# Swin attention and a dynamic convolution: the parameter stage and step 2 rearranged

## The chip, the cores and the metric

The kernel runs on one core of a Trainium2 chip. A core has a matrix engine (TensorE, "PE" in the profile, its weight loads "PEld"), three engines for elementwise work (VectorE "DVE", ScalarE "ACT", GpSimd "POOL"), a Sync engine that here only issues transfers ("SPq" is its queue), and 16 DMA engines that carry the transfers. Every engine runs its own instructions in the order in which they were written, and waits where one needs what another engine or a transfer has yet to deliver. The metric is the time of one execution on the device in microseconds (us), as a median of runs. Everything is in float32.

## The reference

The input is a batch of 16 images of 192 channels, 56 x 56. The first layer is a Swin block: layer norm over channels, windows of 7 x 7 on an image rolled by 3, attention with 6 heads of 32, a projection, a residual; then a second layer norm, an MLP 192 -> 768 -> 192 with GELU, and a residual. The second layer makes four 3 x 3 taps per channel and image out of the pooled image and convolves with them.

```python
h = _ln(transpose(x), norm1_g, norm1_b)
win = windows(roll(h, (-3, -3)))                       # 64 windows of 49 tokens
q, k, v = split(win @ qkv_w + qkv_b)
attn = softmax(q * SCALE @ k.T + bias[None] + mask)    # bias: relative positions; mask: rolled edges
x1 = x + roll(unwindows(attn @ v @ proj_w + proj_b), (3, 3))
y = gelu(_ln(x1, norm2_g, norm2_b) @ fc1_w + fc1_b) @ fc2_w + fc2_b
x2 = x1 + y
wt = (relu(batchnorm(mean(x2) @ w1.T)) @ w2.T + b2) * MASK     # per image and channel
out = depthwise_conv(x2, wt) + bias
```

## The kernel before, in words

**Tiling.** Channels lie on the partitions: `x0` holds channels 0 to 127, `x1` channels 128 to 191 twice, for the two halves of an image. A step `i` takes one window row of each half of an image, 784 tokens; an image has 4 steps (`STEPS`), all 64 (`NS`). The loop `for i in range(2, NS + 2)` is a software pipeline: in one turn it does the MLP of step i - 2, the attention of step i, the q, k, v of step i + 1 and the norm statistics of steps i + 2 and i - 1. What stands ahead of the loop, from line 852 on, loads parameters, folds norm gains, means and shifts into the weights, and takes steps 0, 1 and 2 through the first stages by hand. The change lies there.

**Order.** `tc.manual_schedule()` leaves every engine's instructions in the order of the text. Waits are put in between by the framework, by tile. Tiles of one tag share buffers.

**Names.** A norm is taken in two parts. `norm_squares` or `norm_folded` make squares (the latter adds the three pieces of a token on POOL first: `xs` is filled by two transfers, `copies`; `sums`, `squares` and `fold` follow). `norm_stats` gets means by matmuls with `sel` into `st`, `st_a`, `st_b` or `st_c`; `norm_vars`, `norm_root` and a reciprocal make 1/deviation in `dev`. `norm_spread` writes it to DRAM (`rows`) and reads it back on all partitions (`dv`). Step 0's is spread by matmuls into `pd` instead ("dv" in the profile). `norm1_scale` multiplies into the window tiles `win`, `norm2_scale` into `yn`.

`shift` multiplies a norm's shift with raw weights, a row of 576 (qkv) or 768 (fc1) numbers in one partition. `turn_row` turns pieces of it into columns, one matmul for each 64 or 128. These are added to `qkb`, `bv` (for qkv) and `f1b` (for fc1).

`biases(r, e)` makes one of four attention bias tables, six VectorE additions of `rel_r` and `mask_t`; `r` is 1 for the last step of an image, which is step 3 at the earliest. `attention_scores` adds a table to the scores and makes softmax in `top` (maximum, exponential) and `share` (sum, division); `attention_turn` transposes it into `pt`, copied to `prt`. `attention_v` makes v in two blocks of PSUM, `attention_v_out` copies these into `vbd`, one half on VectorE and one on ScalarE. `attention_qk` returns four copies, q, k and two for the rest, to be called later. `mlp_first` writes `ph`, and has the statistics `st` in its middle; `mlp_wide` and `mlp_narrow` write `pf`. PSUM is four pairs of banks, which all these tiles share in turn.

Of the kernel before, what the change touches and what calls it, by code (L numbers as in the profile page):

```python
# [19 lines left out]
N = WS * WS  # L20
# [16 lines left out]
def tile_swin_then_dynamic_conv(  # L37
# [45 lines left out]
    def banks(name, k):  # L83
        return psum.tile([128, 2, 512], F32, tag=f"pair{k}", name=name)

    def mm(dst, lhs, rhs, start, stop):
        nc.tensor.matmul(dst, lhs, rhs, start=start, stop=stop, skip_group_check=True)  # L87
# [105 lines left out]
    def turn_row(dst, row, lo, n):  # L193
        mm(dst, row[:, lo : lo + n], ident[0:1, 0:1], True, True)

# [9 lines left out]
    qkb = const.tile([128, 3], F32, tag="qkb", name="qkb")  # L205
    wp0 = const.tile([128, DIM], F32, tag="wp0", name="wp0")
# [3 lines left out]
    f1b = const.tile([128, NFC], F32, tag="f1b", name="f1b")  # L210
    wf2 = const.tile([128, NFC, DIM], F32, tag="wf2", name="wf2")
# [27 lines left out]
    mask_t = one.tile([PW, 2, 2, N], F32, tag="prt", name="mask_t", bufs=4)  # L239
# [104 lines left out]
    def norm_vars(keys, st, tag="dev"):  # L344

        lo, hi = min(keys) * 32, max(keys) * 32 + 32
        d = one.tile([128, T], F32, tag=tag, name=f"dev_{keys[min(keys)]}")
        part = d[64 + lo : 64 + hi]
        nc.scalar.activation(part, st[lo:hi, 0, :T], AF.Square)
        nc.vector.tensor_tensor(part, st[64 + lo : 64 + hi, 0, :T], part, ALU.subtract)  # L350
        return part, d
# [4 lines left out]
    def norm_spread(keys, part, tags=("dv1", "sq01"), order=(1, 0)):  # L356

        rows = dram.tile([2 * len(keys), T], F32, tag="rows", name=f"rows_{keys[min(keys)]}")
        nc.sync.dma_start(rows, part[::16])
        out = {}  # L360
        for side in order:
            if side not in keys:
                continue
            v = one.tile([128, 2, T], F32, tag=tags[side], name=f"dv_{keys[side]}")
            at = 2 * (side - min(keys))
            nc.sync.dma_start(
                v,
                rows[at : at + 2].rearrange("(o h) t -> o h t", o=1).broadcast_to([128, 2, T]),
            )
            out[side] = v  # L370
        return out
# [141 lines left out]
    def attention_v_out(pvs):  # L513

        for blk, pv in enumerate(pvs):
            src = pv.rearrange("p h (w n) -> p h w n", w=2)[:, :, :, 0:DIM]
            src = src.rearrange("p h w (g j d) -> p h w g j d", j=2, d=HD)
            for h, copy in enumerate((nc.vector.tensor_copy, nc.scalar.copy)):
                for s in range(2):
                    for j in range(2):  # L520
                        dst = vbd[h][j * 64 : j * 64 + N].rearrange(
                            "p (b w s) g (j d) -> p b w s g j d", b=2, s=2, j=2
                        )[:, blk, :, s, :, j, :]
                        copy(dst, src[s * 64 : s * 64 + N, h, :, :, j, :])  # L524
# [352 lines left out]
    load_rows(*images[0], 0, 3 * WS, HALF, nc.sync)  # L877
    nc.sync.dma_start(rawf[:, 0], fc1_w[0:C0])
    rows2(rawf[:, 1], fc1_w, nc.sync)
# [9 lines left out]
    nc.sync.dma_start(mask_t, win_mask)  # L889
# [31 lines left out]
    g1, be1, bq, bk, bv = columns(*rows1, 2, nc.vector.tensor_copy)  # L921
    nc.vector.memset(kbd, 0.0)
# [16 lines left out]
    part, _ = norm_vars(keys, st, "o")  # L939
# [4 lines left out]
    pq = banks("qkb_p", 2)  # L944
    row = shift(pq, raw, 3 * DIM, be1, "qkb_row")
    pq = pq[:, 0, 384:390]
    norm_squares("1_2", 2, 1, nc.scalar)

    pd = banks("dv_0", 3)
    for h in range(2):  # L950
        pick_row = ident[64:96, 64 + h * 16 : 65 + h * 16].broadcast_to([32, 128])
        mm(pd[:, h, :T], pick_row, part, True, True)
    fold_center(wqkv, 3 * DIM, pm)
# [8 lines left out]
    for _, c, at, lo, n, _ in parts:  # L962
        turn_row(pq[at : at + n, c : c + 1], row, lo, n)
    g2, be2, f2b, pb, cb = columns(*rows3, 1, nc.scalar.copy)
    norm1_scale(0, pd[:, :, :T], nc.vector)
    for dst, c, at, _, n, b in parts:
        nc.vector.tensor_tensor(dst, b, pq[at : at + n, c : c + 1], ALU.add)
# [3 lines left out]


    st = banks("st_b", 0)
    keys = {0: "1_1", 1: "1_2"}
    norm_stats(keys, {0: 1, 1: 2}, st)
    part, _ = norm_vars(keys, st)
# [5 lines left out]
    for r in range(2):  # L982
        for e in range(2):
            biases(r, e)
# [35 lines left out]
    pbp, f1p, pt = pv[:, 0, 384:386], pv[:, 0, 392 : 392 + NFC], pv[:, 1, 384:512]  # L1020
    top(0)
    row = shift(pv, rawf, HID, be2, "f1b_row")

    def rows_to_columns():
        for f in range(NFC):
            turn_row(f1p[:, f : f + 1], row, f * 128, 128)

    qs[1], outs = attention_qk(1, 2, 0, 1, rows_to_columns, nc.vector)
# [29 lines left out]
    outs[3]()  # L1058
    o = attention_rows(0, attention_values(0, prts, 3, 2))
# [36 lines left out]
    dvs.update(norm_spread(keys, part))  # L1096
# [9 lines left out]
    v_whole()  # L1106
    copies, sums_, squares, fold = norm_folded("1_4", 4, 0)
    copies()
    squares(nc.scalar)()
    table(AF.Gelu)  # L1110
    sums_((0,))
    yns[0] = norm2_scale(0, dvs.pop(1), True)
    sums_((1,))
    fold()
    attention_v_out(pvs)
# [245 lines left out]
```

## Time and profile before

The three runs took 3045.3, 3045.47 and 3048.54 us. The profiled execution has a span of 3044.4 us.

| Engine | busy, us | share |
| --- | --- | --- |
| TensorE (PE) | 3022.7 | 99% |
| VectorE (DVE) | 2156.3 | 71% |
| ScalarE (ACT) | 1948.7 | 64% |
| GpSimd (POOL) | 1343.5 | 44% |

In the page, a group's line gives code line, engine, operation, tiles written and read, count, busy time and mean of one, and idle time of its engine before it with what ended most of that. In a timeline, each line starts with the time from the start of the span and the duration, and ends with the idle time before it in brackets. Lines of a matmul are those of a helper, L87, so that tiles tell them apart; a float32 matmul shows as two records. In a table of stretches, each engine has its busy time and, in brackets, the number of its instructions; then come the TensorE clock that was granted (1 is full), the mean busy share of the DMA engines, and what they moved.

### The profile page before, as it was taken

How to read it: one execution, taken by the hardware profiler on the slowest of the kernel's cores; microseconds unless marked ns; L12 is line 12 of the kernel's file. 1: busy time of each engine (PE TensorE's matmuls, PEld its weight loads, DVE VectorE, ACT ScalarE, POOL GpSimd, SP SyncE). 2: the span in 40 equal slices, each digit the busy share in tenths (PEclk: the TensorE clock that was granted, in tenths of full speed). 3: DMA queues.
4: the chain of work that ended last, by engine and by line, in shares of the span. 5: the costliest groups of instructions: out<-in, count | busy, mean ns of one | idle time of the engine just before them, and what ended most of it. 6: DMA issues, size and time to landing. Idle time of an engine off the chain costs nothing.

```text
span 3044.4 us, 62149 instructions
## 1 busy us (share of the span) xinstructions
PE 3022.7 (99%) x25174; PEld 1891.4 (62%) x25174; DVE 2156.3 (71%) x3841; ACT 1948.7 (64%) x3159; POOL 1343.5 (44%) x1269
## 2 busy tenths in 40 slices
PE   9999999999999999999999999999999999999998
PEld 5666666666666666666666666666666666666654
DVE  8656677676686676776866867767767668668664
ACT  4666676666666666766766667667666667666563
POOL 6444534444435445344444444453454444444422
PEclk9999999999999999999999999999999999999999
DMA  4112121111211112121121211212111121211101
GB/s 111 33 31 59 41 75 41 43 60 46 73 38 62 52 44 68 44 72 36 41 67 47 70 36 52 65 41 78 39 47 56 46 73 38 62 52 43 33 30 56
DMA packets 68711, 159.89 MB, mean 53 GB/s; under 512 B 11250, under 2 KB 35288, under 8 KB 66504
## 3 DMA queue, kind: packets, MB, share of 16 engines
q1 hardware_dynamic: 66766, 153.84, 16.7%
q8 instruction: 199, 3.26, 0.4%
q0 software_dynamic: 1360, 1.26, 0.3%
q14 instruction: 88, 0.72, 0.1%
q10 hardware_dynamic: 298, 0.81, 0.1%
HBM read 92.24 MB, written 38.93 MB: 43 GB/s over the span
## 4 chain that ended last, share of the span: by engine, by line
PE 97%; DVE 1%; DMA 1%; POOL 1%; issue 0%; ACT 0%; SPq 0%; POOLq 0%; DVEq 0%; ACTq 0%
PE ph L87 26%; PE pf L87 25%; PE pv L87 8%; PE pp L87 8%; PE po L87 6%; PE pq L87 5%; PE pt L581 5%; PE sc L87 4%; PE pk L87 4%; PE pe L87 4%; PE st L87 2%; PE pc L87 0%; DMA wp<-in_L_conv_proj_w_dram 0%; PE pb_p L87 0%; DVE e L559 0%
## 5 line engine op out<-in xcount | busy, mean ns | idle before, releaser
L87 PE MATMUL pf<-hid,wf 128*128 128x392 f32 (+1 forms) x3072 | 802.6, 493 | 1.5 <-DVE e L552 1.5
L87 PE MATMUL ph<-yn,wf 128*128 128x392 f32 (+1 forms) x3072 | 799.3, 497 | 1.8 <-ACT vbd L524 1.5
L568 POOL TENSOR_TENSOR prob<-e,tot 113x588 f32<-113x588 f32 x256 | 298.3, 1176 | 1098.8 <-DVE tot L567 1098.6
L87 PEld LDWEIGHTS ph<-yn,wf 128*128 128x128 f32 (+1 forms) x3072 | 426.4, 188 | 346.6 <-issue 47.5
L87 PEld LDWEIGHTS pf<-hid,wf 128*128 128x128 f32 (+1 forms) x3072 | 386.2, 164 | 301.3 <-issue 120.2
L524 ACT COPY vbd<-pv 49x192 f32<-49x192 f32 x512 | 160.5, 313 | 575.9 <-DVE vbd L524 571.4
L717 DVE SCALAR_TENSOR_TENSOR x<-pf,cols,x 128x784 f32<-128x784 f32 (+1 forms) x128 | 106.2, 830 | 506.3 <-PE pf L87 447.6
L671 ACT ACTIVATE hid<-ph,f1b 128x784 f32<-128x784 f32 x384 | 337.2, 913 | 133.7 <-PE ph L87 132.2
L781 DVE SCALAR_TENSOR_TENSOR y<-x,wt,y 128x770 f32<-128x770 f32 x282 | 287.7, 1030 | 15.3 <-ACT y L773 7.0
L87 PEld LDWEIGHTS pv<-wqkv,win 64*128 64x128 f32 (+1 forms) x2048 | 255.4, 188 | 31.4 <-issue 1.2
L87 PE MATMUL pv<-wqkv,win 64*128 64x192 f32 (+1 forms) x2048 | 272.5, 325 | 0.3 <-DVE kbd L470 0.3
L559 DVE TENSOR_TENSOR e<-e,top 113x588 f32<-113x588 f32 x256 | 262.3, 1025 | 8.9
L293 POOL TENSOR_TENSOR xs<-x,x 64x392 f32<-64x392 f32 x246 | 249.1, 1013 | 34.4 <-DVE x L657 25.1
L87 PE MATMUL pp<-o,wp 128*128 128x392 f32 (+2 forms) x896 | 251.4, 514 | 0.0
L587 ACT COPY prt<-pt 128x678 f32<-128x678 f32 x256 | 179.2, 727 | 111.6 <-PE pt L581 110.1
L259 ACT ACT_TABLE_LOAD x192 | 246.3, 1283 | 5.3 <-issue 1.8
L562 ACT ACTIVATE e<-e 113x588 f32<-113x588 f32 x256 | 177.1, 692 | 109.7 <-DVE e L559 109.7
L552 DVE TENSOR_TENSOR e<-sc,bias_t 113x588 f32<-113x588 f32 x256 | 179.5, 762 | 60.6 <-PE sc L87 59.5
L415 POOL TENSOR_TENSOR yn<-x,dv 128x784 f32<-128x784 f32 x62 | 115.8, 1867 | 234.0 <-DMA dv<-rows 234.0
L581 PEld LDWEIGHTS pt<-ident,prob 113*128 113x128 f32 x1536 | 165.4, 141 | 64.9 <-issue 35.1
L87 PE MATMUL po<-prt,vbd 128*64 128x49 f32 x6144 | 196.8, 223 | 0.2 <-ACT prt L587 0.2
L87 PEld LDWEIGHTS po<-prt,vbd 128*64 128x64 f32 x6144 | 188.8, 138 | 9.4 <-ACT prt L587 0.5
(186 smaller groups left out, 4429.3 us busy)
## 6 DMA issues: line engine op xcount, KB each, us to landing
dv<-rows SPq DMA_DIRECT2D x127, 392.0 KB
xs<-x SPq DMA_DIRECT2D x246, 98.0 KB
x<-in_x_dram SPq DMA_DIRECT2D x15, 1484.0 KB
out_dram<-y SPq DMA_DIRECT2D x46, 392.0 KB
out_dram<-y SPq DMA_DIRECT2D x48, 196.0 KB
x<-in_x_dram SPq DMA_DIRECT2D x15, 392.0 KB
x<-in_x_dram SPq DMA_DIRECT2D x15, 350.0 KB
out_dram<-y SPq DMA_DIRECT2D x16, 308.0 KB
```

Source lines behind the costliest of these rows:

```text
L87: nc.tensor.matmul(dst, lhs, rhs, start=start, stop=stop, skip_group_check=True)
L259: nc.scalar.activation(junk, eps_t[0:1], func)
L293: nc.gpsimd.tensor_tensor(xs[p, 0], v0[p, h], v1[p], ALU.add)
L524: copy(dst, src[s * 64 : s * 64 + N, h, :, :, j, :])
L552: nc.vector.tensor_tensor(e, sc[:PW, :, : HEADS * N], rel, ALU.add)
L559: nc.vector.tensor_tensor(ehs[wp], ehs[wp], t.broadcast_to([PW, 2 * HEADS, N]), ALU.subtract)
L562: nc.scalar.activation(es[wp], es[wp], AF.Exp)
L568: nc.gpsimd.tensor_tensor(prob[wp][:PW, :, 0:N], ehs[wp], t.broadcast_to([PW, 2 * HEADS, N]), ALU.mult)
L581: nc.tensor.transpose(pt[:, a, g * PW : (g + 1) * PW], prob[wp][:PW, h : h + 2, :].rearrange("p h k -> p (h k)"), ident[:PW, :PW],)
L587: nc.scalar.copy(prt, pt[:, :, : 3 * PW])
L671: nc.scalar.activation(hid[:, f], phs[f][:, :, :T], AF.Gelu, bias=f1b[:, f : f + 1])
L781: nc.vector.scalar_tensor_tensor(dst, src, wt[:, kc, t : t + 1], dst, ALU.mult, ALU.add)
```

## The change

It has five parts.

- `dev` of step 0 becomes a whole tile `d0`, zeroed ahead; the two matmuls that spread it take all 128 rows instead of 32.
- The turns of the shift rows go from TensorE to transfers: six for qkv into a new tile `pq`, six for fc1 into `f1p`, all on the Sync queue. There they stand ahead of the loads of fc1's weights and of step 3's rows, which go later.
- `st_b`, the statistics of steps 1 and 2, moves ahead of the columns of the second parameter group; step 2's squares go ahead of `shift`; the additions to the biases go behind `norm_vars`.
- The two bias tables of an image's last step are made later, one after step 1's q, k and one in step 2. `mask_t` takes a buffer of tag `y` for that, and is loaded earlier.
- In step 2, v is copied out ahead of the squares of step 4: block 0 before the scaling of step 0 for its MLP, block 1 after it. The second read of 1/deviation goes behind the transfers for `xs`.

The purpose is to keep TensorE on full and uninterrupted work from the first products on, and to take work that is not yet needed out of the way of the first steps.

```diff
@@ -190,9 +190,6 @@
         nc.scalar.copy(row, dst[0:1, :, : n // 2])
         return row.rearrange("o c n -> o (c n)")
 
-    def turn_row(dst, row, lo, n):
-        mm(dst, row[:, lo : lo + n], ident[0:1, 0:1], True, True)
-
     ident = const.tile([128, 128], F32, tag="ident", name="ident")
     eps_t = const.tile([128, 1], F32, tag="eps", name="eps_t")
     junk = const.tile([1, 1], F32, tag="junk", name="junk")
@@ -203,11 +200,13 @@
 
     wqkv = const.tile([128, 2, 3 * DIM], F32, tag="wqkv", name="wqkv")
     qkb = const.tile([128, 3], F32, tag="qkb", name="qkb")
+    pq = const.tile([128, 5], F32, tag="pq", name="pq")
     wp0 = const.tile([128, DIM], F32, tag="wp0", name="wp0")
     wp1 = const.tile([128, C0], F32, tag="wp1", name="wp1")
     wp2 = const.tile([128, 128], F32, tag="wp2", name="wp2")
     wf1 = const.tile([128, 2, HID], F32, tag="wf1", name="wf1")
     f1b = const.tile([128, NFC], F32, tag="f1b", name="f1b")
+    f1p = const.tile([128, NFC], F32, tag="f1p", name="f1p")
     wf2 = const.tile([128, NFC, DIM], F32, tag="wf2", name="wf2")
 
 
@@ -236,7 +235,7 @@
     raw_all = one.tile([128, 2, 3 * DIM + HID], F32, tag="hid", name="raw")
     raw, rawf = raw_all[:, :, 0 : 3 * DIM], raw_all[:, :, 3 * DIM :]
     rel_r = work.tile([PW, N, HEADS], F32, tag="y", name="rel_r", bufs=3)
-    mask_t = one.tile([PW, 2, 2, N], F32, tag="prt", name="mask_t", bufs=4)
+    mask_t = work.tile([PW, 2, 2, N], F32, tag="y", name="mask_t", bufs=3)
 
 
     def rows_of(i):
@@ -341,10 +340,11 @@
             which, src = streams[at][k]
             mm(st[at * 32 : at * 32 + 32, 0, :T], sel[:, which], src, k == 0, k == n - 1)
 
-    def norm_vars(keys, st, tag="dev"):
+    def norm_vars(keys, st, d=None):
 
         lo, hi = min(keys) * 32, max(keys) * 32 + 32
-        d = one.tile([128, T], F32, tag=tag, name=f"dev_{keys[min(keys)]}")
+        if d is None:
+            d = one.tile([128, T], F32, tag="dev", name=f"dev_{keys[min(keys)]}")
         part = d[64 + lo : 64 + hi]
         nc.scalar.activation(part, st[lo:hi, 0, :T], AF.Square)
         nc.vector.tensor_tensor(part, st[64 + lo : 64 + hi, 0, :T], part, ALU.subtract)
@@ -357,18 +357,19 @@
 
         rows = dram.tile([2 * len(keys), T], F32, tag="rows", name=f"rows_{keys[min(keys)]}")
         nc.sync.dma_start(rows, part[::16])
-        out = {}
-        for side in order:
-            if side not in keys:
-                continue
+
+        def read(side):
             v = one.tile([128, 2, T], F32, tag=tags[side], name=f"dv_{keys[side]}")
             at = 2 * (side - min(keys))
             nc.sync.dma_start(
                 v,
                 rows[at : at + 2].rearrange("(o h) t -> o h t", o=1).broadcast_to([128, 2, T]),
             )
-            out[side] = v
-        return out
+            return v
+
+        if order is None:
+            return read
+        return {side: read(side) for side in order if side in keys}
 
     def norm1_scale(i, dv, engine):
 
@@ -510,9 +511,10 @@
 
         return pvs, rest, whole
 
-    def attention_v_out(pvs):
-
-        for blk, pv in enumerate(pvs):
+    def attention_v_out(pvs, blks=(0, 1)):
+
+        for blk in blks:
+            pv = pvs[blk]
             src = pv.rearrange("p h (w n) -> p h w n", w=2)[:, :, :, 0:DIM]
             src = src.rearrange("p h w (g j d) -> p h w g j d", j=2, d=HD)
             for h, copy in enumerate((nc.vector.tensor_copy, nc.scalar.copy)):
@@ -874,9 +876,7 @@
     rows2(raw[:, 1], qkv_w, nc.sync)
     load_rows(*images[0], 0, WS, 2 * WS, nc.sync)
     load_rows(*images[0], 0, 2 * WS, 3 * WS, nc.sync)
-    load_rows(*images[0], 0, 3 * WS, HALF, nc.sync)
-    nc.sync.dma_start(rawf[:, 0], fc1_w[0:C0])
-    rows2(rawf[:, 1], fc1_w, nc.sync)
+    nc.sync.dma_start(mask_t, win_mask)
     nc.vector.memset(wp2, 0.0)
     nc.vector.memset(rel_r, 0.0)
     rows3 = columns_load(
@@ -886,7 +886,6 @@
         nc.gpsimd,
     )
 
-    nc.sync.dma_start(mask_t, win_mask)
 
     side = 2 * WS - 1
     for j in range(2):
@@ -919,6 +918,8 @@
 
 
     g1, be1, bq, bk, bv = columns(*rows1, 2, nc.vector.tensor_copy)
+    d0 = one.tile([128, T], F32, tag="o", name="dev_0")
+    nc.vector.memset(d0, 0.0)
     nc.vector.memset(kbd, 0.0)
     norm_squares("1_0", 0, 0, nc.scalar, ("yn0", "q4"))
     fold_scale(
@@ -936,21 +937,13 @@
     st = banks("st_a", 3)
     keys = {0: "1_0"}
     norm_stats(keys, {0: 0}, st)
-    part, _ = norm_vars(keys, st, "o")
+    part, _ = norm_vars(keys, st, d0)
     norm_root(part)
     nc.vector.reciprocal(part, part)
     norm_squares("1_1", 1, 0, nc.scalar)
     pm = fold_means(wqkv, 3 * DIM, "fq", 0)
-    pq = banks("qkb_p", 2)
-    row = shift(pq, raw, 3 * DIM, be1, "qkb_row")
-    pq = pq[:, 0, 384:390]
     norm_squares("1_2", 2, 1, nc.scalar)
-
-    pd = banks("dv_0", 3)
-    for h in range(2):
-        pick_row = ident[64:96, 64 + h * 16 : 65 + h * 16].broadcast_to([32, 128])
-        mm(pd[:, h, :T], pick_row, part, True, True)
-    fold_center(wqkv, 3 * DIM, pm)
+    row = shift(banks("qkb_p", 2), raw, 3 * DIM, be1, "qkb_row")
     parts = (
         (qkb[:, 0:1], 0, 0, 0, 128, bq[0]),
         (qkb[:, 1:2], 1, 0, DIM, 128, bk[0]),
@@ -960,28 +953,35 @@
         (bv[1][0:64], 4, 0, 2 * DIM + 128, 64, bv[1][0:64]),
     )
     for _, c, at, lo, n, _ in parts:
-        turn_row(pq[at : at + n, c : c + 1], row, lo, n)
+        nc.sync.dma_start(pq[at : at + n, c : c + 1], row[:, lo : lo + n])
+    nc.sync.dma_start(rawf[:, 0], fc1_w[0:C0])
+    rows2(rawf[:, 1], fc1_w, nc.sync)
+    load_rows(*images[0], 0, 3 * WS, HALF, nc.sync)
+
+    pd = banks("dv_0", 3)
+    for h in range(2):
+        pick_row = ident[:, 64 + h * 16 : 65 + h * 16].broadcast_to([128, 128])
+        mm(pd[:, h, :T], pick_row, d0, True, True)
+    fold_center(wqkv, 3 * DIM, pm)
+
+    st = banks("st_b", 0)
+    keys = {0: "1_1", 1: "1_2"}
+    norm_stats(keys, {0: 1, 1: 2}, st)
     g2, be2, f2b, pb, cb = columns(*rows3, 1, nc.scalar.copy)
     norm1_scale(0, pd[:, :, :T], nc.vector)
+    part, _ = norm_vars(keys, st)
     for dst, c, at, _, n, b in parts:
         nc.vector.tensor_tensor(dst, b, pq[at : at + n, c : c + 1], ALU.add)
     nc.vector.tensor_scalar(qkb[:, 0:1], qkb[:, 0:1], SCALE, None, ALU.mult)
     nc.vector.tensor_scalar(qkb[0:64, 2:3], qkb[0:64, 2:3], SCALE, None, ALU.mult)
     nc.vector.tensor_scalar(kb, pick, qkb[:, 1:2], None, ALU.mult)
-
-
-    st = banks("st_b", 0)
-    keys = {0: "1_1", 1: "1_2"}
-    norm_stats(keys, {0: 1, 1: 2}, st)
-    part, _ = norm_vars(keys, st)
     norm_root(part)
     table(AF.Exp)
     nc.vector.reciprocal(part, part)
     dvs.update(norm_spread(keys, part, tags=("dv1", "yn0"), order=(0, 1)))
     images[1] = load_x(1, nc.sync)
-    for r in range(2):
-        for e in range(2):
-            biases(r, e)
+    for e in range(2):
+        biases(0, e)
     nc.gpsimd.dma_start(wp0, proj_w[0:C0])
     rows2(wp1, proj_w[:, 0:C0], nc.gpsimd)
     for h in range(2):
@@ -1017,15 +1017,12 @@
 
     top, share = attention_scores(0, *qs.pop(0), (3, 2, 0, 1))
     pv = banks("pb_p", 3)
-    pbp, f1p, pt = pv[:, 0, 384:386], pv[:, 0, 392 : 392 + NFC], pv[:, 1, 384:512]
+    pbp, pt = pv[:, 0, 384:386], pv[:, 1, 384:512]
     top(0)
     row = shift(pv, rawf, HID, be2, "f1b_row")
-
-    def rows_to_columns():
-        for f in range(NFC):
-            turn_row(f1p[:, f : f + 1], row, f * 128, 128)
-
-    qs[1], outs = attention_qk(1, 2, 0, 1, rows_to_columns, nc.vector)
+    for f in range(NFC):
+        nc.sync.dma_start(f1p[:, f : f + 1], row[:, f * 128 : (f + 1) * 128])
+    qs[1], outs = attention_qk(1, 2, 0, 1, None, nc.vector)
 
     mm(pbp[:, 0:1], wp0[:, 0:C0], bv[0], True, False)
     mm(pbp[:, 0:1], wp1[0:64], bv[1][0:64], False, True)
@@ -1056,6 +1053,7 @@
     prts = [attention_turn(0, wp, (2, 1)[wp % 2]) for wp in range(4)]
     outs[2]()
     outs[3]()
+    biases(1, 0)
     o = attention_rows(0, attention_values(0, prts, 3, 2))
 
 
@@ -1093,7 +1091,8 @@
     norm_root(part)
     outs[1]()
     nc.vector.reciprocal(part, part)
-    dvs.update(norm_spread(keys, part))
+    read = norm_spread(keys, part, order=None)
+    dvs[1] = read(1)
     prts = [attention_turn(1, wp, (2, 0)[wp % 2]) for wp in range(4)]
 
     s, m, g, b = (bn[:, k] for k in range(4))
@@ -1104,15 +1103,19 @@
     pvs, v_rest, v_whole = attention_v(2, (0, 1))
     v_rest()
     v_whole()
+    biases(1, 1)
     copies, sums_, squares, fold = norm_folded("1_4", 4, 0)
     copies()
-    squares(nc.scalar)()
+    rest = squares(nc.scalar)
+    sums_((0,))
+    attention_v_out(pvs, (0,))
+    yns[0] = norm2_scale(0, dvs.pop(1), True)
+    dvs[0] = read(0)
+    attention_v_out(pvs, (1,))
+    rest()
     table(AF.Gelu)
-    sums_((0,))
-    yns[0] = norm2_scale(0, dvs.pop(1), True)
     sums_((1,))
     fold()
-    attention_v_out(pvs)
     pp, pair1, p_narrow, p_rest, p_whole = project(1, o, 3, 2)
     p_narrow()
     p_rest()
```

## The prediction

> **What bounds the kernel now.** I read the page first, then the stretches of the first 110 us, then the timelines of single engines, then TensorE's waits. The page says where time can be had at all:
>
> ```profile
> span 3044.4 us, 62149 instructions
> PE 3022.7 (99%) x25174; PEld 1891.4 (62%) x25174; DVE 2156.3 (71%) x3841; ACT 1948.7 (64%) x3159; POOL 1343.5 (44%) x1269
> PE 97%; DVE 1%; DMA 1%; POOL 1%; issue 0%; ACT 0%; SPq 0%; POOLq 0%; DVEq 0%; ACTq 0%
> ```
>
> Outside TensorE there are 22 us in the whole run, and none of the edits touches the 25 us of `pf` and `ph` matmuls per step (802.6 + 799.3 us over 64 steps) that make up half of the rest. What is won or lost before TensorE enters its closed stream, at about 105 us, is carried to the end one for one. So the question is when the products of step 0's MLP (`ph`, then `st`) run. Four places set that. First, the stretches (columns: PE busy, loads, DVE, ACT, POOL, granted clock, DMA share, GB/s):
>
> ```profile
> 14.00:16.00 2.00, 2.00 (x8) 0.91 (x7) 1.96 (x4) 0.35 (x1) 1.81 (x4) 1.00 1.07 244
> 16.00:18.00 2.00, 2.00 (x16) 1.62 (x14) 0.77 (x2) 1.46 (x3) 2.00 (x4) 0.78 1.04 256
> 18.00:20.00 2.00, 2.00 (x16) 1.03 (x20) 1.88 (x10) 0.17 (x1) 1.33 (x4) 0.50 0.78 141
> 20.00:22.00 2.00, 2.00 (x17) 0.39 (x8) 1.20 (x12) 0.00 (x0) 0.76 (x2) 0.50 0.29 38
> 22.00:24.00 2.00, 2.00 (x10) 0.87 (x8) 0.57 (x1) 0.66 (x2) 2.00 (x4) 0.52 0.46 46
> 24.00:26.00 2.00, 2.00 (x12) 1.01 (x9) 1.52 (x1) 1.94 (x3) 2.00 (x3) 1.00 0.91 18
> ```
>
> TensorE is granted half its clock from 17.1 to 23.9 us. Its timeline shows what ran then, and just before:
>
> ```profile
> 15.54 1.25 PE L87 MATMUL dv<-dev,ident 32*128 32x392 f32 x3
> 16.68 1.55 PE L87 MATMUL qkb_p<-ident,qkb_row 1*128 1x1 f32 x9
> 18.47 0.87 PE L87 MATMUL st_b<-x,sel 128*32 128x392 f32 x2
> 22.55 1.59 PE L87 MATMUL pq<-win,wqkv 64*128 64x392 f32 x4
> ```
>
> Ahead of the drop stand products on 32 rows and one-column turns: nearly empty work. After it `st_b` takes a step every 0.65 us, where `st` at 104.75 takes one every 0.35. Second, VectorE and ScalarE around 27 to 51 us:
>
> ```profile
> 27.11 5.67 DVE L911 TENSOR_TENSOR bias_t<-rel_r,mask_t 113x98 f32<-113x98 f32 x24
> 32.80 2.95 DVE L524 COPY vbd<-pv 49x192 f32<-49x192 f32 x8
> 46.99 0.69 ACT L562 ACTIVATE e<-e 113x588 f32<-113x588 f32 x1 [2.19 <-DVE e L559]
> 51.08 1.35 ACT L587 COPY prt<-pt 128x678 f32<-128x678 f32 x2 [0.79 <-PE pt L581]
> ```
>
> Third, around 92 us, ScalarE's and POOL's timelines and TensorE's:
>
> ```profile
> 92.22 0.53 ACT L302 ACTIVATE sq<-xs 128x392 f32<-128x392 f32 x1 [4.30 <-DMA xs<-x]
> 95.14 2.58 ACT L524 COPY vbd<-pv 49x192 f32<-49x192 f32 x8
> 94.74 1.01 POOL L314 TENSOR_TENSOR sq<-sq,sq 128x392 f32<-128x392 f32 x1
> 103.33 1.18 POOL L315 TENSOR_TENSOR sq<-sq 128x392 f32<-128x392 f32 x1
> 96.45 8.37 PE L87 MATMUL ph<-yn,wf 128*128 128x392 f32 x36 [1.53 <-ACT vbd L524]
> 104.75 0.52 PE L87 MATMUL st<-xs,sel 128*32 128x392 f32 x2
> ```
>
> ScalarE waits 4.3 us for a transfer before its squares, and TensorE then waits 1.5 us for the copies behind them. But see the last two: POOL ends its folding at 104.51, and `st` starts at 104.75, when `ph` is just through. POOL has no slack there.
>
> **What the Trainium skill says.** "TensorE: Matmul & The Clock Gate", part 1, what's actually happening: TensorE falls to half clock after a window of about 3.4 us in which it was idle, and comes back after a busy one. The trace agrees, with two such windows at 0.50 (6.8 us); that emptiness, not only idleness, brings the drop is my reading of the rows above. "DMA: Bandwidth & Descriptors", anatomy of one DMA: some 2 us are fixed, mostly the receipt; here `rows<-dev` takes 1.65. "SBUF — State Buffer", who interferes with whom: a VectorE operation with two SBUF inputs contends with POOL's reads; here POOL's fold takes 1.01 at 95 us and 1.29 at 102, beside VectorE's scaling.
>
> **The change, part by part.** Times are on the clock of before.
>
> Full rows and no turns in the prologue. `dv` becomes four full-row matmuls of 0.33, 15.54 to about 17.0; no turns follow, `st_b` comes at once, and the clock stays at 1. `st_b` is six steps of 0.33 instead of 0.65: 2.0 us, done at 18.9. Then the queue's next is `pq`, which needs VectorE's scaling of step 0: that began at 17.23, after `dv`, and ended at 20.33; now 17.0 to 20.1. `pq` starts at 20.2 instead of 22.55 (2.35). The three short products before 25.39 run warm, 2.08 instead of 2.84 (0.75). The long ones start 3.1 us earlier, at 22.3. The memset of d0 (some 0.35 us, from 2.02 us for six times the elements) lies in a VectorE wait for the weights that ends at 8.79.
>
> Transfers in their place. Six issues on the Sync queue at 0.58 (as for x rows), from 16.28: out at 19.8. Landing: 1.65 (`rows`) to 4.8 us (`rel_r`, software queue) later, so 21.4 to 24.6; I take 21.7. Behind them on that queue stand fc1's weights and step 3's rows, nine issues of half a us, done by 24.7, first needed at 34 and 46. VectorE's bias additions wait for the landing, and behind these on VectorE the reciprocal (2.6), half the bias tables (2.83) and the copies of v, which can't start before 29.5. So a landing up to 23.2 costs nothing; 24.6 costs 1.4.
>
> Bias tables. 12 of 24 operations leave the chain, 2.83 us. But the v copies are then held by TensorE: the last v product of their block ended at 32.60, 0.2 us before they started. So of 2.83 only 0.2 is cashed here: copies 32.60 + 0.06 - 3.1 = 29.56, a gain of 3.24. The other twelve lie in VectorE idle times of 2.56 (before 57.11) and 3.63 us (before 90.94), 1.42 each: nothing.
>
> fc1's turns. 12 matmuls, 43.17 to 44.60, leave TensorE: 1.43. It is then 4.67 ahead. But the softmax of step 0 is VectorE work without a gap from 35.78 to 48.78; that moves by 3.24, and ScalarE's last exponential with it (46.99 to 43.75). Behind that in ScalarE's queue stand q and k of step 1 (0.90 and 1.90) and then `prt`: 47.2 instead of 51.08. **So 3.9 us arrive here**, and every later stage to 90 us hangs on it. fc1's six transfers leave at 38 to 42 and are wanted at 45: hidden.
>
> v ahead of the squares in step 2. v's first block is ready at 89.8: VectorE copies to 91.3, ScalarE to 92.6; VectorE's norm2 scaling (dv landed 90.94) 91.3 to 93.25; second block VectorE to 94.75, ScalarE to 96.05. `ph` starts when `pp` is through, at 94.77 instead of 96.45: 1.7 gained. The new wait: the squares (1.5 us) now end at 97.55 instead of 93.71. POOL stands still for them from 94.78, with fold of step 4, squares, sums and fold of step 1 queued behind. It had fold at 94.74 and the end at 104.51, 0.49 of it a wait for a transfer that is hidden now. So fold starts at 97.6 and the end is 97.6 + 9.77 - 0.49 = 106.9, `st` 107.1. TensorE, ready at 103.1, stands 4 us. **Against before that is 2.35 later, not 1.7 earlier.** The long products behind `st` are 2.35 late as well. And 4 us of standing is longer than the skill's window, so I expect a second stretch at half clock: 0 to 2.8 us, and 1.3 taken (one window with some 2.6 us of work in it).
>
> Sum: -3.9 + 2.35 + 1.3 = -0.25 us, 3045.2; I say 3045.
>
> **The rivals.** (a) The forecast, no difference: 3043.9 (no second half-clock stretch) to 3046.7 (2.8). 0.55. (b) POOL's wait does not bite, because ScalarE's squares get in earlier or POOL runs faster without its neighbour: 3045.5 - 3.9 - 1.7 = 3039.9. For it: ScalarE is idle 4.3 us there. Against: the squares stand behind copies that wait for VectorE. 0.24. (c) As (b), and ScalarE's queue before `prt` doesn't hold back the 0.8: 4.67 + 1.7, or more, gives 3039.1 and below, past the bound of 6.1 us. 0.09. (d) Slower: transfers land late (1.4), TensorE cools in the prologue all the same (some 3 of the 3.9 lost), and step 2 costs 2.35 + 2.8: 3045.5 - 3.9 + 1.4 + 3 + 5.15 = 3051.2; half of these, 3048.3. Against it: `st_b` and `pq` fill the window that was empty. 0.12, of which 0.05 over the bound.
>
> **How the numbers follow.** The range takes (a), (b) and the milder half of (d): 3039.3 to 3049.5. Faster by over 0.2% (6.1 us) is (c) and a little of (b): 0.11. Slower is 0.05. The rest, 0.84, is within.
>
> **What would show it.** Right: clock 1.00 in every stretch from 11 to 30 us; `pq` near 20.2; the first `prt` copy near 47.2; `ph` some 5.5 us earlier than 96.45; a TensorE wait of 3 to 4 us at `st` put down to POOL, perhaps with a clock under 1 behind it; nothing different from 130 us on but the shift. Wrong: no wait at `st` (then b), half clock still at 18 to 24 us, or VectorE waiting for `pq`'s transfers after 23 us (then d).

## The result and the profile after

The changed kernel takes 3053.07 us (median; 3052.01 to 3057.81) against 3045.57 (3045.3 to 3048.54) for the kernel before, measured side by side: ratio 1.0026, 95% interval 1.0013 to 1.0038. It is slower by some 7.5 us, where no difference was forecast. The profiled execution has

```profile
span 3054.0 us, 62117 instructions
PE 3025.9 (99%) x25150; PEld 1891.8 (62%) x25150; DVE 2165.2 (71%) x3842; ACT 1947.4 (64%) x3159; POOL 1342.9 (44%) x1269
```

TensorE is as full as before and only 3.2 us busier. Held against before, the first `sc` product of step 2 starts 7.01 us later (116.71 for 109.70) and that of step 63 by 7.22 (2951.85 for 2944.63), so the repeated steps between them lose next to nothing. The loss is made ahead of 117 us, as the forecast said that any gain would be. At the end this execution adds some 1.5 us at step 63, where a transfer for `xs` landed late (eight of the 16 profiles of this study show a wait of 0.3 to 1.5 there; why is open), and 1.25 us in the last convolution, which has more half clock.

Stretches of the changed kernel (same columns as the table of before):

```profile
16.00:18.00 2.00, 2.00 (x19) 0.74 (x21) 1.17 (x5) 0.05 (x1) 2.00 (x5) 1.00 0.36 99
20.00:22.00 2.00, 1.96 (x12) 1.76 (x12) 1.34 (x9) 1.35 (x2) 2.00 (x5) 1.00 0.45 37
38.00:40.00 2.00, 2.00 (x18) 0.75 (x10) 1.40 (x3) 1.03 (x2) 1.85 (x5) 0.50 0.97 406
```

and the last of these in before:

```profile
38.00:40.00 2.00, 2.00 (x6) 0.72 (x6) 1.97 (x3) 0.91 (x2) 1.77 (x8) 1.00 1.00 208
```

The clock is 1.00 at 17 to 24 us, where it was 0.50, as forecast, and `pq` starts at 20.04 (forecast 20.2). But 10.2 us of half clock now stand at 34.9 to 45.2, where before had none. VectorE's timeline shows what came between:

```profile
22.06 5.30 DVE L977 TENSOR_SCALAR kb<-pick,qkb 128x2 f32<-128x2 f32 x1
27.40 2.60 DVE L980 RECIPROCAL dev<-dev 64x392 f32<-64x392 f32 x1
```

One multiplication of 128 x 2 numbers takes 5.30 us. In before the same line takes

```profile
21.10 0.21 DVE L970 TENSOR_SCALAR kb<-pick,qkb 128x2 f32<-128x2 f32 x1
```

Now POOL's timelines, of the changed kernel and of before:

```profile
21.91 2.71 POOL L997 MEMSET vbd<- 128x1536 f32 x2
24.54 2.80 POOL L997 MEMSET prob<- 128x768 f32 x4
```

```profile
23.29 2.71 POOL L997 MEMSET vbd<- 128x1536 f32 x2
25.92 2.80 POOL L997 MEMSET prob<- 128x768 f32 x4
```

The changed `kb` starts 0.15 us after the first of six memsets, and ends (27.36) when the last one does (27.34). In before it was through 2 us ahead of them. What hangs on it is seen on ScalarE of the changed kernel:

```profile
27.46 1.91 ACT L467 ACTIVATE kbd<-pk,kb,pick 128x784 f32<-128x784 f32 x2 [2.54 <-DVE kb L977]
53.45 1.35 ACT L589 COPY prt<-pt 128x678 f32<-128x678 f32 x2 [0.69 <-PE pt L583]
```

k waits 2.54 us for `kb`, the reciprocal starts at 27.40 (before 24.48), TensorE finds neither k nor v and stands between its `sc` products (1.38 and 2.07 us), and half clock follows. The first `prt` copy is at 53.45, 2.37 us later than before, not 3.9 earlier.

Step 2 of the changed kernel, on ScalarE, POOL and TensorE:

```profile
98.75 0.53 ACT L301 ACTIVATE sq<-xs 128x392 f32<-128x392 f32 x1
```

```profile
100.31 1.04 POOL L313 TENSOR_TENSOR sq<-sq,sq 128x392 f32<-128x392 f32 x1 [4.92 <-ACT sq L308]
```

```profile
107.10 0.52 PE L87 MATMUL st<-xs,sel 128*32 128x392 f32 x1 [0.49 <-POOL xs L294]
110.30 1.52 PE L87 MATMUL st<-sq,sel 128*32 128x392 f32 x2 [2.35 <-POOL sq L314]
111.74 5.04 PE L87 MATMUL ph<-yn,wf 128*128 128x392 f32 x12
```

Here the forecast's chain stands link by link: squares late, POOL still for 4.92 us, TensorE waiting 0.49 + 2.35 us at `st`, and half clock behind it (110.0 to 113.4), in which the rest of `ph` takes 5.04 us for 4.22.

### The profile page after: what moved, and what is told of

The parts are those of the page before. It is cut to its first block, busy times and chain, and to the rows that moved or that the text cites. A ratio compares the mean times of both kernels' runs of the same rounds, so it can differ in the third digit from the quotient of the medians.

```text
span 3054.0 us, 62117 instructions
## 1 busy us (share of the span) xinstructions
PE 3025.9 (99%) x25150; PEld 1891.8 (62%) x25150; DVE 2165.2 (71%) x3842; ACT 1947.4 (64%) x3159; POOL 1342.9 (44%) x1269
## 3 DMA queue, kind: packets, MB, share of 16 engines
q0 software_dynamic: 1360, 1.26, 0.3%
## 4 chain that ended last, share of the span: by engine, by line
PE 96%; DVE 2%; POOL 1%; issue 0%; DMA 0%; SPq 0%; ACT 0%; POOLq 0%; DVEq 0%; ACTq 0%
PE ph L87 25%; PE pf L87 25%; PE pv L87 8%; PE pp L87 8%; PE po L87 6%; PE pq L87 5%; PE pt L583 5%; PE sc L87 4%; PE pk L87 4%; PE pe L87 4%; PE st L87 2%; PE pc L87 0%; PE pb_p L87 0%; DVE e L561 0%; DVE vbd L526 0%
```

## Experiments

Each kernel was timed in five rounds beside the kernel before, on the same chip. Single spans of one kernel spread over 5 us and more, so a ratio has an interval of about 0.0008 to either side (2.4 us), and traces decide what times leave open. The groups e1 to e4, e5 to e8, e9 to e12 and e13 with e14 each had a chip of their own, so across groups only the ratios are compared.

**kb in two columns (e1).** The changed kernel with

```diff
-    nc.vector.tensor_scalar(kb, pick, qkb[:, 1:2], None, ALU.mult)
+    for h in range(2):
+        nc.vector.tensor_scalar(kb[:, h : h + 1], pick[:, h : h + 1], qkb[:, 1:2], None, ALU.mult)
```

> The changed kernel, with the one two-column operation that makes kb written as two one-column operations. Theory: that operation took 5.30 us because VectorE had to wait for POOL's memsets of vbd and prob (21.91 to 27.34 us), and everything up to the first prt copy hangs on it, with the half-clock stretch of 34.9 to 45.2 us as a consequence. Then the two operations take under 0.4 us together, the reciprocal behind them starts near 22.4 us instead of 27.40, the half-clock stretch goes, the first prt copy comes near 47.3 us instead of 53.45, and the time falls by some 6 us to 3047. Rival 1: the operation was slow for what it reads (columns that transfers have just delivered): then the two operations together take as long, and the time stays at 3053. Rival 2: the delay is hidden by later waits: kb is quick, but the time stays at 3053.

Measured: 3051.45 us, ratio to before 1.0013 (1.0007 to 1.0020), where the changed kernel had 1.0026. The two operations take 0.19 us each beside the same memsets, the reciprocal starts at 22.07, no half clock at 35 to 45, first `prt` 49.04, `ph` 92.75. The wait at `st` stays. So the theory of what held `kb` came true, but not its size: the time was to fall to 3047, and `prt` to 47.3.

**Step 2 in its old order (e2), and both (e3).** The changed kernel with the two reads of 1/deviation side by side again (not shown) and with

```diff
-    rest = squares(nc.scalar)
+    squares(nc.scalar)()
+    table(AF.Gelu)
     sums_((0,))
-    attention_v_out(pvs, (0,))
     yns[0] = norm2_scale(0, dvs.pop(1), True)
-    dvs[0] = read(0)
-    attention_v_out(pvs, (1,))
-    rest()
-    table(AF.Gelu)
     sums_((1,))
     fold()
+    attention_v_out(pvs)
```

> The changed kernel, with step 2 in the order of before: squares ahead of the copies of v, both reads of 1/deviation at once. Theory: the new order makes POOL wait for the squares and TensorE for POOL; it cost 3.4 us (POOL's end is 5.73 us later than before, of which 2.37 came in with the first prt copy) and another 1.2 us at half clock. Then st follows ph with no wait over 0.3 us, clock 1.00 there, and the time falls by 4.6 us to 3048.5. Rival: the new order gains the 1.5 us that ph waited for v's copies, and the loss is all in the prologue: then the time rises by 1 to 1.7 us, to 3054.5.

> The changed kernel with both of the edits: kb in two operations and step 2 in the order of before. Theory: the two costs are separate and add: 3053.1 - 6 - 4.6 = 3042.5, 3 us below before, which is what the prologue's edits are worth by themselves. Rival: they are one cost seen twice (a late TensorE meets POOL either way): then it is no better than the better of the two alone, 3047.

Measured: e2 3049.52, ratio 1.0008 (1.0000 to 1.0017); its `kb` took 3.80 us and again ended with the memsets (26.58 and 26.56). e3 3046.73, ratio 1.0000 (0.9992 to 1.0008), with no wait at `st`. The two losses add up: some 3 us for `kb`, some 4 to 5 for step 2. And they are all that the times show: what is left of the change has no gain over 0.0008, so not the 3.9 us of the forecast, which the theory of e3 still counted in part (3042.5).

**Step 2's new order alone (e4).** The same diff the other way round, on the kernel before.

> The kernel before with only the new order of step 2 (copies of v ahead of the squares, the second read of 1/deviation later); the bias tables stay where they were. Theory: ph starts 1.7 us earlier, POOL's folds end 2.4 to 3.4 us later than 104.51, TensorE stands at st for about 4 us, and a window at half clock follows: 3045.6 + 2.4 to 4.6 = 3048.0 to 3050.2. Rival: the reorder by itself is a gain, and it is the rest of the change that makes it meet POOL: 3043.9.

Measured: 3051.32, ratio 1.0017 (1.0010 to 1.0024): slower without any of the other parts, by 4.6 us in the medians, the upper end of what was expected. TensorE's waits in it have

```profile
PE st L87 <- POOL sq L315: 2.3, 1, 2.3
```

the same 2.3 us as in the changed kernel, and 6.8 us of half clock from 109.2.

**POOL's memsets earlier (e5).** This leaves `kb` alone and moves what it was thought to collide with:

```diff
+    for t in (*vbd, *prob):
+        nc.gpsimd.memset(t, 0.0)
     nc.gpsimd.dma_start(wp0, proj_w[0:C0])
...
-    for t in (*vbd, *prob):
-        nc.gpsimd.memset(t, 0.0)
```

> The changed kernel with POOL's memsets of vbd and prob moved ahead of the loads of wp, so that they run some 6 us earlier; the 128 x 2 multiplication that makes kb is untouched. Theory (kb is held by POOL's memsets as long as these follow one another): kb takes about 0.2 us again, the reciprocal behind it starts at 22 to 23 us, no half clock at 35 to 45 us, first prt copy near 49, time about that of the kernel with kb in two columns, some 1.5 to 2 us under the changed kernel (3051 to 3051.5, ratio 1.0013). Rival (kb is slow for what it reads or for the transfers behind its operand): it still takes 3.8 to 5.3 us, and the time is that of the changed kernel, 3053 (ratio 1.0025).

Measured: 3052.45, ratio 1.0021 (1.0012 to 1.0030). VectorE's timeline has

```profile
22.89 0.36 DVE L977 TENSOR_SCALAR kb<-pick,qkb 128x2 f32<-128x2 f32 x1
```

with the memsets at 14.30 to 19.73. So it is the memsets that held `kb`. The time missed its mark, because at their new place they hold another small operation of VectorE, a copy that takes 0.18 us in the changed kernel:

```profile
15.88 3.90 DVE L138 COPY cols_rows<-cols_rows 5x64 f32<-5x64 f32 x1
```

It ends at 19.78, again with the last memset. Step 0's scaling stands behind it (`pq` at 21.53 for 20.0 in e1, half clock at 22.6), and the wait at `st` is still there.

**Squares between the copies (e6).** Step 2 once more, with `kb` in two columns:

```diff
     attention_v_out(pvs, (0,))
+    rest()
     yns[0] = norm2_scale(0, dvs.pop(1), True)
     dvs[0] = read(0)
     attention_v_out(pvs, (1,))
-    rest()
```

> kb in two columns, and in step 2 ScalarE's three squares placed between its copy of v's block 0 and its copy of block 1, the rest as in the changed kernel. Theory (the step 2 loss comes from POOL's fold waiting for squares that stand behind block 1's copy, which waits for VectorE's scaling): the squares run in a time when ScalarE is idle, POOL's fold starts 2 us or more earlier against ph than in the kernel with kb in two columns, TensorE's wait at st falls from 2.9 to under 1 us and no half clock follows it; ph stays near 93 us; time 3044 to 3046. Rival (what costs is the early copies of v as such, or POOL's fold is slower beside its neighbours): the wait at st stays at 2 us or more and the time at 3050 to 3052.

Measured: 3046.77, ratio 1.0002 (0.9994 to 1.0010), where e1 has 1.0013, some 3.4 us less. On POOL and on TensorE:

```profile
95.38 1.01 POOL L313 TENSOR_TENSOR sq<-sq,sq 128x392 f32<-128x392 f32 x1 [1.38 <-ACT sq L308]
```

```profile
95.83 8.61 PE L87 MATMUL ph<-yn,wf 128*128 128x392 f32 x36
104.37 0.52 PE L87 MATMUL st<-xs,sel 128*32 128x392 f32 x2
```

POOL's fold starts 0.45 us ahead of `ph` instead of 2.9 behind it, and `st` follows `ph` without a wait. From `ph` to the next `sc` are 13.49 us; before has 13.25, the changed kernel 19.31, e1 19.51. That confirms the cause of the step 2 loss. But `ph` was to be near 93, as in e1, and is at 95.83: this execution has half clock at 40.1 and 70.8, and e1, with the same instructions up to there, had none.

**Two tries at the prologue's lost gain (e8, e9).** Both are e6 with fc1's and step 3's loads elsewhere on the Sync queue: in e8 ahead of qkv's turns, where before has them, in e9 behind the writing and reading of 1/deviation.

> As the kernel with kb in two columns and the squares between the copies, and with the loads of fc1's weights and of step 3's rows ahead of the qkv turns on the Sync queue again, as before. Theory (the gain in the prologue is given back because step 1's 1/deviation, written and read behind those loads, lands late, so that POOL scales step 1 late): dv of step 1 lands 1.5 us or more earlier than with the loads behind, TensorE's wait for POOL's win falls from 2.9 to 1 us or less, time about 1 us under the kernel without this edit. Rival (the landing is set by the chain ahead of it on VectorE, or the DMA engines are full either way): dv lands at the same time and the time is equal; and the turns, now behind the loads, may land late and hold VectorE.

> As the kernel with kb in two columns and the squares between the copies of v, with the loads of fc1's weights and of step 3's rows moved behind the writing and reading of step 1's and 2's 1/deviation on the Sync queue (still ahead of the second image). Theory (what the prologue wins is given back because dv of step 1 stands behind 1 MB of loads on the Sync queue, so that POOL scales step 1 late and TensorE waits 2.0 us for it): rows is issued as soon as the reciprocal ends, near 26.2 instead of 27.6, POOL's win starts at 31 to 32 instead of 33.4, TensorE's wait at pq of step 1 falls to under 1 us, the first prt copy comes 1.5 to 2.5 us before 49.0, time 3043 to 3045. Rival (the late loads hold fc1's products and step 3's squares instead, or the DMA engines are full either way): POOL's win stays within 0.5 us, or a new wait for raw or x appears, and the time stays at 3046 to 3047.

Measured: e8 3048.96, ratio 1.0008 (1.0000 to 1.0016): the end of the rival came true, the turns landed late; VectorE waits 4.64 us for `pq`, and the reciprocal starts at 27.84. e9 3047.29, ratio 1.0003 (0.9995 to 1.0011): POOL's `win` does start at 31.42 instead of 33.39, and the first `prt` at 47.48. But fc1's turns then stand behind the second image on that queue, and VectorE has

```profile
51.48 0.17 DVE L1049 TENSOR_TENSOR f1b<-f1b,f1p 128x6 f32<-128x6 f32 x1 [4.51 <-DMA f1p<-f1b_row]
```

so that TensorE waits 2.1 us for `w1t` behind it. Neither gains.

**Full rows alone (e7), and before with a filled tail (e12).** e7 is before with `d0` and the two full-row products, the turns left on TensorE. e12 is before with five products that nothing uses, ahead of the last convolution (the prologue is untouched):

```diff
             convs.append({"b": b, "n": 0})
+            if i > NS:
+                fp = banks("fill", B_)
+                for j in range(5):
+                    mm(fp[:, j % 2, :T], ident, wf2.rearrange("p f n -> p (f n)")[:, 0:T], True, True)
```

> The kernel before with only the first part done: d0 is a whole zeroed tile and the two matmuls that spread it take all 128 rows; the turns stay on TensorE. Theory (half clock at 17 us comes of the window of 32-row products and one-column turns together, and of the latter most): the one-column turns still follow, so half clock comes again, at about the same place or a little later, and the time is within 1 us of before. Rival (the 32-row products alone bring it): clock 1.00 to 30 us, pq near 21 instead of 22.55, and the first prt copy 1 to 2 us earlier than 51.08.

> The kernel before with the same five unused products ahead of the last convolution and nothing else. Theory (as for the other filled kernel): no half clock at 3027 to 3034 us, time 1.5 to 3.5 us under before. Rival: half clock stays, time equal.

Measured: e7 3047.10, ratio 1.0001 (0.9993 to 1.0009). Its clock stays at 1.00 to 50 us, with the turns still there, so the theory stated for it did not come true, and `prt` comes at 48.90; no time is gained. e12 3044.74, ratio 0.9995 (0.9987 to 1.0003). What it shows in its prologue was not expected at all. Its stretches and TensorE's timeline:

```profile
16.00:18.00 2.00, 2.00 (x25) 1.54 (x27) 1.15 (x3) 1.25 (x3) 2.00 (x4) 1.00 1.09 266
18.00:20.00 2.00, 1.90 (x25) 0.63 (x19) 1.81 (x11) 0.12 (x1) 1.28 (x3) 1.00 0.55 89
```

```profile
19.88 1.04 PE L87 MATMUL pq<-win,wqkv 64*128 64x392 f32 x4
```

These are the instructions of before, 32-row products and turns included, at full clock: `pq` at 19.88 instead of 22.55, `prt` at 48.82 instead of 51.08. It is more than half of the forecast's 3.9 us at `prt`, without the change. Nor is it carried on: in e7 and e12 `ph` starts at 96.29 and 97.51, about where before has it (96.45) or later, behind half clock at 50 us (in e12 at 70 too) and a longer wait for the copies of v (2.04 and 1.75 us for 1.53).

**What is left, on before (e10, e13, e14), and the filled tail on e9 (e11).** e10 is before with full rows and with step 2's early copies, squares between. e13 is e10 with the filled tail, e14 the same without full rows.

> The kernel before with two parts alone: full rows for dv of step 0 (turns kept on TensorE), and in step 2 the early copies of v with the squares between block 0's and block 1's copy. Theory (full rows keep the clock, worth 2 us at the first prt copy; early v with squares between is worth 1.5 us at ph and leaves no wait at st): ph at 93.5 to 95 against 96.45, no wait of TensorE at st over 0.5 us, time 1 to 3 us under before. Rival (the stages between 50 and 95 us have limits of their own, on VectorE or in a half-clock stretch, which take the gain again): ph within 0.7 us of 96.3 and the time within 1 us of before.

> The kernel before with full rows for dv of step 0, the early copies of v with the squares between, and the five unused products ahead of the last convolution. Theory (what is left of the change once its two losses are out, and the filled tail, add up): 3042 to 3043.5, ratio 0.9986 to 0.9992, faster than both kernels; no wait at st, no half clock from 3020 us until the last products end. Rival (each was worth nothing and the difference was chance): 3045 to 3046, ratio 0.9997 to 1.

> The same without the full rows, so that the prologue is that of before, products on 32 rows and turns on TensorE. Theory (the half clock at 17 us in the profile of before came of where the clock's raster of 3.41 us lay in that one execution, and full rows are worth nothing): the time is within 1 us of the kernel with full rows; in this profile half clock at 17 us appears only if an edge of the raster falls near 17.1 us, and pq starts near 19.9 where it doesn't. Rival (full rows keep the clock in most executions): 1 to 2 us slower than the kernel with full rows, half clock at 15 to 19 us in the profile wherever the edge falls.

> As the kernel with the spread first, and with five products of 128 rows by 392 columns that nothing uses put into the 3 us in which TensorE waits for dg ahead of the last convolution. Theory (half clock follows a stretch of 3.4 us of the clock's raster in which TensorE did little): no half clock after 3024 us until the last products end, the last convolution's products 1.7 to 3.4 us shorter, and the time 1.5 to 3.5 us under the same kernel without the filling. Rival (the clock drops there for another cause, such as the load of the stretch before): half clock stays and the time is equal or longer.

Measured: e10 3044.71, ratio 0.9995 (0.9987 to 1.0003); e13 3044.47, 0.9997 (0.9989 to 1.0005); e14 3044.03, 0.9991 (0.9983 to 0.9999); e11 3047.13, 1.0001 (0.9993 to 1.0009), no gain over e9 in the time. The gains expected of e13 (to 3043.5 or less) and of e11 over e9 (1.5 us or more) do not show in the medians, and e10's (1 to 3 us) is within the noise. e14, before with two small edits, is the only one of 14 whose interval lies under 1, and barely, which can be chance. Its profile has the old prologue again, and the half clock again:

```profile
18.00:20.00 2.00, 2.00 (x16) 0.94 (x19) 1.88 (x10) 0.17 (x1) 1.40 (x3) 0.50 0.87 169
```

In every profile of this study all changes of the clock lie on a raster of 3.41 us, whose place against the start of the kernel differs from one execution to the next:

| profile | edges of the raster near there, us | array filled in the cell before each edge | half clock at 17 us | `pq`, us | first `prt`, us |
| --- | --- | --- | --- | --- | --- |
| before | 17.10 | 39% | yes | 22.55 | 51.08 |
| e4, same prologue | 17.09 | 40% | yes | 22.77 | 51.28 |
| e14, same prologue | 17.03 | 39% | yes | 22.46 | 51.00 |
| e12, same prologue | 15.91 and 19.32 | 49%, 55% | no | 19.88 | 48.82 |
| e7, full rows | 15.82 and 19.23 | 59%, 55% | no | 20.34 | 48.90 |
| e10, full rows | 16.32 and 19.73 | 68%, 55% | no | 20.13 | 48.71 |
| e9, full rows and no turns | 17.02 | 72% | no | 19.92 | 47.48 |
| e11, full rows and no turns | 17.27 | 82% | no | 19.42 | 46.41 |

"TensorE: Matmul & The Clock Gate", part 1, says that the window is free-running and doesn't start with the kernel; all 16 profiles agree. The prediction read the window's length there, not that. Where a cell of the raster covered 13.7 to 17.1 us of the old prologue, half clock came; where it ended at 15.91, it didn't. The expectation of e14 had said so before its run: half clock only with an edge near 17.1.

The third column is counted from the traces. In each cell TensorE's matmul records are added up, each by its columns times the share of the 128 x 128 array that its weights cover, and the sum is given as a share of the median cell of the repeated steps. From 10 us on, in all 16 profiles, 34 cells at full clock were followed by half clock, and none of them was over 41%; of the 14,110 cells that were not followed, ten were as low. Busy time does not part them: in before TensorE was busy through its whole cell. The count was made afterwards, and five cells ahead of 10 us, the first at full clock in their profiles, do not fit it.

From it comes an estimate. Slid along the timeline of e12, with its end anywhere from 14 to 22 us, a cell of the old prologue is that low when it ends between 16.6 and 18.7 us, 2.1 of 3.41 us; so roughly half of the executions of before, or somewhat more, would have this half clock. With full rows (e7, e10, e13) no such place of the cell is under 46%, and with the turns gone too (changed kernel, e1, e3, e9) none under 53%. The last two rows of the table agree with that: there part 1 of the change does what it is meant to. e7 alone, with its edge at 15.82, could not have told. But neither e7 nor e13 against e14 shows a gain in the median that the intervals can tell.

The tail gives the clock's other test. TensorE's timelines of before and e12 have

```profile
3027.28 12.36 PE L87 MATMUL pc<-x,dg 128*128 128x392 f32 x32 [3.09 <-POOL dg L1272]
```

```profile
3025.21 3.52 PE L87 MATMUL fill<-wf,ident 128*128 128x392 f32 x10
3028.57 10.56 PE L87 MATMUL pc<-x,dg 128*128 128x392 f32 x32
```

With the 3 us filled no half clock stands ahead of `pc` in e11, e12, e13 or e14, and the last convolution's products take 10.56 us for 12.36. The twelve profiles without the filling all have half clock there. The 1.5 to 3.5 us that the whole kernel was to gain by it are not shown: 1.3 in e12, within its interval, and none in e11 over e9.

## Why the prediction was wrong

**Full rows and no turns in the prologue: right in this trace, too large as a gain.** Clock 1.00 from 11 to 30 us, `st_b` at 0.33 a step, `pq` at 20.04, long products at 22.33: all within 0.2 us. But the 2.35 and 3.1 us were counted against one profile of before, in which the raster lay so that half clock came. The same code has `pq` at 19.88 in e12. "That emptiness, not only idleness, brings the drop" was one half of it; where the raster lies is the other half.

**Turns by transfer: right.** Last landing 21.86 (forecast 21.7), a wait of 0.56 us on VectorE. The fixed two us that the prediction cites stand in the page's section on transfers that GpSimd issues; these went on the Sync queue, and the last, issued from 19.2 on, was there at 21.86.

**The chain on VectorE behind it: this is the first step that failed.** "VectorE's bias additions wait for the landing, and behind these on VectorE the reciprocal" put no cost on what stands between them. `kb` took 5.30 us for 0.21, because its new place fell into POOL's memsets, which themselves moved 1.4 us earlier (23.29 to 21.91). The reciprocal came at 27.40, not 22.3, the copies of v at 32.91, not 29.56. The page cited for contention, "SBUF — State Buffer", who interferes with whom, also says that `tensor_scalar` can enter a mode that takes the port pair shared with GpSimd, and that the one that comes second is then fully blocked. The trace agrees in what it shows (5.30, 3.80 and, for a copy, 3.90 us, each to the end of the memsets; 0.36 without them). That it is this mode is the page's explanation; why forms of one column were not held stays open. In one point the trace goes further: the page has the pair taken for one instruction, but `kb`, which came after the first, waited for all six. I had priced this contention for POOL's fold only.

**"So 3.9 us arrive here": the second step that failed.** With `kb` mended, `prt` is at 49.04 in e1 and at 47.81 in e3, with the same instructions up to there: 2.0 and 3.3 us before the 51.08 of before, but 0.2 after and 1.0 before the 48.82 of e12. ScalarE's queue was not the limit: in e1 POOL scaled step 1 at 33.55, no earlier than before (33.66) and 3 us later than e12 (30.52), and TensorE waited 2.0 us. `dv` stood behind fc1's and step 3's loads, which part 2 had moved on the Sync queue. Their nine issues, counted as done by 24.7, ran to 26.04 in e1, and `rows` went out 2.35 us behind the reciprocal; in e9, with the loads behind it, at once. I had called those loads hidden, asking when they are needed and not who stands behind them. Nor does "every later stage to 90 us hangs on it" hold as it stands: in e3 2.5 of the 3.3 us are gone again at `ph` (95.65 for 96.45), with half clock at 49 and 69 us.

**Bias tables and fc1's turns.** That the first half of the tables cashes nothing of its own fits e3, where nothing of the rest shows in the time; no run took these edits alone.

**Step 2: the mechanism right, the size near.** Forecast: 1.7 us gained at `ph`, lost again, 2.35 more at `st`, 1.3 by the clock, so 5.35 us more between `ph` and the next `sc`; the trace shows 6.06 (19.31 for 13.25). The wait of 1.53 us at `ph` is gone in the changed kernel and 0.40 in e4, so most of the 1.7 us was there; where `ph` stands on the clock depends on the half clock ahead of it as well (96.45 in before, 97.51 in e12, 92.75 in e1).

**The sum.** -3.9 became +2.37 at `prt`, and from there to the `sc` of step 2 the forecast's 3.65 became 4.64: together the 7.01 us. The rival on the slower side reached 3051.2. It named late landings, which did not come, and a TensorE that cools in the prologue, which came at 35 us and by way of `kb`; the step 2 loss, its third part, came. That `kb` would be held was in no case.

## What to carry to other kernels

Before half clock in one profile is booked as a gain, find the raster's edges in that profile and ask whether the low stretch would still fill a cell if the raster lay elsewhere; if not, the gain comes in some executions only, and may be gone again at a later stage. When an instruction moves in time, look at what the other engine that shares its ports does at the new time, and price small operations too: 256 numbers cost 5 us here. When a transfer moves on a queue, ask who stands behind it, not only when it is needed itself.

## What was not expected of the hardware

- A `tensor_scalar` of 128 x 2 float32 was held for 5.30 us by six back-to-back memsets on GpSimd and not let in between two of them; a copy of 5 x 64 was held for 3.90 us in the same way (e5). `tensor_scalar` forms of one column beside the memsets took 0.13 to 0.19 us.
- With `f1p` in SBUF instead of PSUM, the addition to `f1b` took 1.26 us beside POOL's squares for 0.15 in before, and 0.17 in e9.
- Half clock came after cells of the raster in which TensorE filled little of its array, 41% or less of a usual cell, whether it stood idle or was busy with small products, and lasted one, two or three cells (3.4, 6.8, 10.2 us). The same count tells most of how long: of the half-clock cells under 39%, 18 of 21 were followed by another, of the 31 over it none.
- In the first 116 us the profiles show between none (e10) and 17.0 us (e4) of half clock; e1 and e6, with the same instructions up to 89 us, show none and 6.8 there. This alone moves single runs of one kernel by some us.
